# Four-layer convolution-style network: matmuls of different row or column tiles queued in groups, replicas in two-bank tiles, PSUM shared by both lanes

## The chip, the cores and the metric

The kernel runs on one core of a Trainium2 chip. The metric is the device time of one execution in microseconds; a kernel is run several times and the median counts. The engines are named as in the profile: PE (TensorE matmuls), PEld (TensorE weight loads), DVE (VectorE), ACT (ScalarE), POOL (GpSimd) and SP (the queue that issues DMA transfers). PSUM is the memory that PE writes; here it holds eight banks of 128 x 512 f32.

## What is computed

The input is 16 images of 56 x 56 positions and 128 channels in f32. Four layers follow one another, each of the form x = x + layer(group_norm(x)):

```
x = x + _L0_conv_ref(_gn(x), ...)   # shifted 7x7 window attention, 4 heads
x = x + _L1_conv_ref(_gn(x), ...)   # layer norm, gated products, l @ r over columns, layer norm
x = x + _L2_conv_ref(_gn(x), ...)   # Fourier layers: attention over heads, three spectral operators
x = x + _L3_conv_ref(_gn(x), ...)   # bilinear: depthwise convolutions and two contractions
```

The parts the change touches, cut to the core. Layer 3:

```
q = l2norm(xp[..., :NH*DK].reshape(b, t, h, NH, DK), -1).reshape(b*t*h, NH, DK)
K_H1 = conv2d(k, H1_w, groups=DK) ... + P1
kernel = jnp.einsum('xnk,xkd->xnd', q, K_H1)
V_G = conv2d(v, G_w) ... + I
feature = jnp.einsum('xvw,xvd->xwd', V_G, feature)
out = jnp.einsum('xnd,xvd->xvn', kernel, feature)
```

Layer 2, of which the change touches the scores over 32 heads, the product of the attention weights with values under a spectral filter, and the inverse transforms:

```
scores = jnp.einsum('bhtd,bhsd->bhts', qs, ks) / ...
out = jnp.einsum('bhts,bhsd->bhtd', softmax(scores), vs)
projd = _fno_layer(out, wP, wPs, bPs, (H, W))
```

Layer 1: two projections of the normed input, each gated by a sigmoid of a third and fourth.

## The kernel before

The image stays in SBUF as 128 channels by 3136 positions (`xt`) through all four layers; nothing but the table of layer 2, a padded copy of the keys and values of layer 3, input and output passes through HBM. The 16 images are written one after the other in the program text, the even ones on lane 0 and the odd ones on lane 1. A lane has its own work area (`arena`), small tiles and PSUM pools, so the framework's scheduler, which fixes the order of each engine's queue when the program is built, lets the two lanes run at the same time: it puts an instruction on its queue when its operands and its tile's buffer are ready by its own reckoning, the older image first. On the chip each queue then runs in that order, and an instruction that waits holds up what stands behind it on its engine.

PSUM before: each lane has two pools (`psp` and `prp`, lines 314 and 315) of two one-bank tiles. `psb` (line 333) takes from them alternately, or from the one that is asked for: in the bilinear stage the accumulators, convolutions and projections use pool 0 and the replicas pool 1.

Every f32 matmul stands in the profile as two LDWEIGHTS and two MATMUL records. A matmul whose operand has 32 rows uses a row tile of the array, and one whose output has 32 or 64 partitions a column tile.

The places that matter:

- `_bilinear`, stage 3, per image seven chunks of 448 positions. `contract` (line 1268 on) computes one of the einsums of layer 3 for a chunk; it is called three times a chunk, so 21 times an image. It runs in two halves `n`. In a half, four matmuls with 32-row operands (line 1277) spread rows of `y` over 128 partitions, the replicas; each replica is multiplied by `z` on DVE (line 1282), or, every third one, copied by ACT (line 1285) and multiplied on POOL (line 1286); then eight matmuls (line 1290), for `h` in two and `i` in four, add products `i` into the column tile 32 `i` of the accumulator. `conv` (line 1264) makes `z` by three matmuls per half of the outputs, and `project` the inputs of the chunk. The products have a ring of five buffers.
- `_fourier`, stage 2. In the loop of line 1086 on, for each of eight slices `q` of the spectrum, 16 pairs of heads are loaded from the table by two DMAs each on SP's queue into a ring of five buffers (line 1096), multiplied by the spectrum (line 1098; every third multiplication on POOL, the rest on DVE), and multiplied by the attention weights into two accumulators (line 1103), pairs with `half` 0 in the upper 64 partitions and `half` 1 in the lower. The accumulators stand from the first to the eighth step of a slice. In `attention` the scores are made by products (line 992, DVE or POOL) and matmuls (line 1001) in the same two halves. `inverse` (line 886) uses four column tiles.
- `_triangle`, stage 1: line 638 makes four columns of the gated projections in one bank, ACT takes the sigmoid (line 648), and DVE multiplies (lines 649 and 650).

Of the kernel before, what the change touches and what calls it, by code (L numbers as in the profile page):

```python
# [35 lines left out]
F32 = mybir.dt.float32  # L36
AF = mybir.ActivationFunctionType
ALU = mybir.AluOpType
# [258 lines left out]
def tile_blocks(ctx: ExitStack, tc: tile.TileContext, ins, out, at, stages=(0, 1, 2, 3)):  # L297
# [6 lines left out]
    def pool(name, bufs, **kw):  # L304
        return ctx.enter_context(tc.tile_pool(name=name, bufs=bufs, **kw))
# [7 lines left out]
    smp = [pool(f"small{k}", 8) for k in range(2)]  # L313
    psp = [pool(f"ps{k}", 2, space=PSUM) for k in range(2)]
    prp = [pool(f"pr{k}", 2, space=PSUM) for k in range(2)]

# [15 lines left out]

    def psb(which=None):

        count[0] += 1
        which = count[0] % 2 if which is None else which
        return (psp, prp)[which][lane[0]].tile([P, 512], F32, tag="ps", name=uid("psb"))

# [9 lines left out]
    ptt = nc.gpsimd.tensor_tensor  # L348
    act = nc.scalar.activation


# [234 lines left out]
def _triangle(env):  # L586
# [27 lines left out]
    def run(b, xt):  # L614
# [17 lines left out]
        for part in range(2):  # L632
            for g in range(T // 4):
                p = e.psb()
                for i in range(4):
                    c0 = (4 * g + i) * T
                    for half, w in ((0, "w1a"), (64, "w1b")):
                        mm(  # L638
                            p[half : half + 64, i * P : (i + 1) * P],
                            lhsT=xh[:, c0 : c0 + 64],  # L640
                            rhs=W(w).rearrange("p (k c) -> p k c", c=64)[:, :, HC * part : HC * part + HC],
                            start=True,
                            stop=True,
                        )
                pv = p.rearrange("p (i c) -> p i c", c=P)
                sg = e.w2()
                s3 = sg[:, :256].rearrange("p (i c) -> p i c", c=64)
                act(s3, pv[:, :, 64:128], AF.Sigmoid)
                tt(l3[:, 4 * g : 4 * g + 4, :], pv[:, :, 0:32], s3[:, :, 0:32], ALU.mult)
                nc.vector.scalar_tensor_tensor(  # L650
                    r3[:, 4 * g : 4 * g + 4, :], pv[:, :, 32:64], 1.0 / T, s3[:, :, 32:64], ALU.mult, ALU.mult
                )
            for g in range(4):
                for half in (0, 64):
                    p = e.psb()
                    s = slice(half, half + T)
                    for c in range(8):
                        mm(p[s, c * T : (c + 1) * T], lhsT=l3[s, :, 8 * g + c], rhs=r3[s, :, 8 * g + c], start=True, stop=True)
                    dst = ot[s, (4 * part + g) * CH : (4 * part + g + 1) * CH]
                    if half:  # L660
                        nc.scalar.copy(dst, p[s, :CH])  # L661
                    else:
                        nc.vector.tensor_copy(dst, p[s, :CH])
# [24 lines left out]
def _fourier(env):  # L688
# [183 lines left out]
    def inverse(parts, consume):  # L872
# [4 lines left out]
        for k in range(2):  # L877
            ng = 4 - k
            vs = []
            for u in range(2):  # L880
                p = e.psb()
                for i in range(4):
# [42 lines left out]
    def attention(uv, ar):  # L925
# [56 lines left out]
        for bank in range(2):  # L982
            sp = e.psb()
            for l0 in (0, 4):
                for c in range(2):
                    prods = []
                    for half in range(2):
# [10 lines left out]
                        prods.append(t4)  # L998
                    for l in range(4):
                        for half, t4 in enumerate(prods):  # L1000
                            mm(  # L1001
                                sp[64 * half : 64 * half + 64, :CH],
                                lhsT=xs[:, l0 + l, :],
                                rhs=t4[:, :, l, :],
                                start=l0 == 0 and c == 0 and l == 0,
                                stop=False,
                            )
            for half in range(2):
# [29 lines left out]
    def run(b, xt):  # L1038
# [47 lines left out]
        for q in range(8):  # L1086
            s = slice(q * STEP, (q + 1) * STEP)
            pa, pb = e.psb(), e.psb()
            acc = [pa[:, :STEP], pa[:, STEP : 2 * STEP], pb[:, :STEP]]
            for two in range(8):  # L1090
                prods = []
                for pair in (2 * two, 2 * two + 1):
# [5 lines left out]
                    engine().tensor_tensor(t3, x3[:, :, s], t3, ALU.mult)  # L1098
                    prods.append(t)
                for p, k, m in ((pa, 0, 2 * STEP), (pb, 2 * STEP, STEP)):  # L1100
                    for half, t in enumerate(prods):
                        pair = 2 * two + half
                        mm(  # L1103
                            p[64 * half : 64 * half + 64, :m],
                            lhsT=at[:, pair % 8, pair // 8, :],
                            rhs=t[:, k : k + m],
                            start=two == 0,
                            stop=two == 7,
                        )
            c0, o = e.w2(), e.w2()  # L1110
            nc.scalar.copy(c0[:, :STEP], acc[0])
# [58 lines left out]
def _bilinear(env):  # L1170
# [13 lines left out]
    def run(b, xt):  # L1184
# [12 lines left out]
        def project(q):  # L1197
# [4 lines left out]
            for t, o, m in ((ha, 0, 128), (hb, 128, 32)):  # L1202
                p = e.psb(0)
                mm(p[:m, :CH], lhsT=W("l3w1")[:, o : o + m], rhs=xg[:, :CH], start=True, stop=True)
                act(t[:m, :CH], p[:m, :CH], AF.Silu)
            p = e.psb(0)
            mm(p[:, :CH], lhsT=W("l3w2a")[:, :P], rhs=ha[:, :CH], start=True, stop=False)
# [4 lines left out]

            p = e.psb(0)
            for a in range(4):
# [19 lines left out]
            )  # L1234
            p = e.psb(0)
            for a in range(4):
# [19 lines left out]
        def conv(w, i, q):  # L1256
# [4 lines left out]
            for h in range(2):  # L1261
                p = e.psb(0)
                for dr in range(3):
# [4 lines left out]
        def contract(y, z, t):  # L1268

            acc = e.psb(0)  # L1270
            for n in range(2):
                done = []
                for two in range(2):
                    ps = [e.psb(1), e.psb(1)]
                    for i, p in enumerate(ps):
                        s = slice(64 * two + 32 * i, 64 * two + 32 * i + 32)
                        mm(p[:, :CH], lhsT=C("rep")[s, n * P : (n + 1) * P], rhs=y[s], start=True, stop=True)  # L1277
                    for p in ps:
                        d = prods[count[1] % 5].rearrange("p (h t) -> p h t", h=2)
# [7 lines left out]
                        done.append(d)  # L1287
                for h in range(2):
                    for i, d in enumerate(done):
                        mm(  # L1290
                            acc[32 * i : 32 * i + 32, :CH],
                            lhsT=C("red")[:, (2 * n + h) * 32 : (2 * n + h + 1) * 32],
                            rhs=d[:, h],
                            start=n == 0 and h == 0,
                            stop=n == 1 and h == 1,
                        )
            nc.scalar.copy(t, acc[:, :CH])
            return t

        def last(q, y):  # L1300
            y = contract(y, conv("l3wg", 1, q), e.w2()[:, :CH])
            p = e.psb(0)
            for a in range(4):
# [7 lines left out]
            )  # L1311
            p = e.psb(0)
            for a in range(4):
# [45 lines left out]
```

## Time and profile before

| what | value |
|---|---|
| runs, us | 20649.91, 20714.76, 20733.38 |
| median, us | 20714.76 |
| profiled execution, us | 20716.84 |
| its span, us | 20715.1 |
| mean granted TensorE clock | 0.807 |
| DVE products L1282 | x1792, 1913.2 us busy, 1089 ns each |
| POOL products L1286 | x896, 1887.4 us busy, 2106 ns each |
| ACT copies L1285 | x896, 476.0 us busy, 531 ns each |
| PE convolutions L1264 | 4032 records, 1877.7 us busy |
| POOL products L1098 | x688, 1167.8 us busy, 1699 ns each |
| DVE products L1098 | x1360, 1372.2 us busy, 1018 ns each |
| DMA arena<-table | x4096, 147.0 KB each |

A group of the profile is one line of the program on one engine: how many records, their busy time (the union of their intervals), the mean duration of one, and the idle time of the engine just before them with what ended most of it. Matmuls that run at the same time count once in the busy time, so busy time over count falls below the mean duration where they overlap. The granted clock is the share of TensorE's full clock that was allowed over a stretch.

After the first two images the program is periodic: two images, one of each lane, take some 2550 us. In the period from 10624 to 13174 us, lane 1 starts an image (window attention from 10624, triangle from 10921, attention of the Fourier layer from 11296, its products from 11420, the bilinear stage from 12406), and lane 0 is half an image ahead (Fourier products from 10647, the bilinear stage from 11402 to 12015, window attention of its next image from 12101, triangle from 12596, attention from 13059). These times are those of the lines 507, 638, 1001, 1103 and 1264 in the trace.

### The profile page before, as it was taken

The page shows a single profiled execution, that of the slowest core. Times are in us where ns is not written, and L with a number is a line of the kernel's source. Part 1 is how long each engine was busy: PE and PEld are TensorE (multiplying, and loading weights), DVE is VectorE, ACT ScalarE, POOL GpSimd, SP SyncE. Part 2 cuts the span into 40 slices and gives each one's busy share as a digit, 9 for nine tenths or more (in the row PEclk, how much of TensorE's full clock was granted, in tenths as well). Part 3 has the DMA queues.
Part 4 walks back from the last instruction along what each step waited for, and adds up shares of the span by engine and source line. Part 5 has one row for each costly group of instructions (what it writes and reads, how often), then busy time and mean ns, then how long its engine had stood idle before and what let it go on. Part 6 is the DMA issues. An engine that isn't in the chain of part 4 may idle for free. (4 is left out here: it accounts for less than half of the span.)

```text
span 20715.1 us, 240603 instructions
## 1 busy us (share of the span) xinstructions
PE 17351.0 (84%) x97248; PEld 8331.4 (40%) x97248; DVE 8795.3 (42%) x14107; ACT 4262.3 (21%) x7720; POOL 4451.6 (21%) x2924
## 2 busy tenths in 40 slices
PE   7888888888888798787987879878798787987968
PEld 4433345344353443534335343353433534334332
DVE  5543344443443434534354343543435434354332
ACT  2212222122121221212212122121221212212111
POOL 0232121221212212122121221212112121122211
PEclk7887888878878788787887878878788787887867
DMA  0220011110111101021010210202002010020100
GB/s 23 78 80 10 8 31 54 59 33 8 46 39 55 37 8 55 29 60 31 8 60 25 60 32 8 67 23 61 25 8 71 22 58 26 8 75 20 57 20 9
DMA packets 477330, 772.15 MB, mean 37 GB/s; under 512 B 118784, under 2 KB 220416, under 8 KB 475008
## 3 DMA queue, kind: packets, MB, share of 16 engines
q1 hardware_dynamic: 476080, 754.54, 12.1%
q8 instruction: 773, 12.66, 0.3%
q14 instruction: 333, 2.73, 0.0%
q10 hardware_dynamic: 144, 2.22, 0.0%
HBM read 709.84 MB, written 33.72 MB: 36 GB/s over the span
## 5 line engine op out<-in xcount | busy, mean ns | idle before, releaser
L1282 DVE TENSOR_TENSOR arena<-psb,arena 128x896 f32<-128x896 f32 x1792 | 1913.2, 1089 | 4070.5 <-PE psb L1277 2140.7
L1286 POOL TENSOR_TENSOR arena<-w,arena 128x896 f32<-128x896 f32 x896 | 1887.4, 2106 | 6633.9 <-ACT w L1285 3359.2
L1290 PE MATMUL psb<-arena,cst 128*32 128x448 f32 x10752 | 2954.4, 640 | 371.0 <-POOL arena L1286 351.7
L1103 PE MATMUL psb<-arena 112*64 112x448 f32 (+1 forms) x8192 | 2452.4, 521 | 379.0 <-DVE arena L1098 303.9
L1277 PE MATMUL psb<-arena,cst 32*128 32x448 f32 x5376 | 2490.3, 648 | 175.7 <-DVE arena L1282 100.2
L1264 PE MATMUL psb<-arena,wgt 113*128 113x448 f32 x4032 | 1877.7, 611 | 225.2 <-DMA arena<-table 149.0
L1098 POOL TENSOR_TENSOR arena<-arena 112x672 f32<-112x672 f32 x688 | 1167.8, 1699 | 3680.8 <-DMA arena<-table 3031.6
L1098 DVE TENSOR_TENSOR arena<-arena 112x672 f32<-112x672 f32 x1360 | 1372.2, 1018 | 1052.7 <-DMA arena<-table 990.9
L1103 PEld LDWEIGHTS psb<-arena 112*64 112x64 f32 x8192 | 887.2, 153 | 1745.2 <-issue 1011.0
L1277 PEld LDWEIGHTS psb<-arena,cst 32*128 32x128 f32 x5376 | 721.9, 202 | 1887.4 <-issue 1148.0
L1290 PEld LDWEIGHTS psb<-arena,cst 128*32 128x32 f32 x10752 | 508.7, 116 | 2401.4 <-issue 1421.6
L1264 PEld LDWEIGHTS psb<-arena,wgt 113*128 113x128 f32 x4032 | 813.5, 214 | 1225.5 <-issue 1097.4
L1285 ACT COPY w<-psb 128x448 f32<-128x448 f32 x896 | 476.0, 531 | 3226.9 <-PE psb L1277 3198.2
L821 POOL TENSOR_TENSOR arena<-arena,sm 128x448 f32<-128x448 f32 x560 | 609.6, 1123 | 1301.2 <-DVE sm L828 1126.4
L1001 PE MATMUL psb<-arena,standing 128*64 128x448 f32 x2048 | 573.7, 646 | 238.5 <-POOL arena L992 118.2
L857 PE MATMUL psb<-cst,arena 128*64 128x32 f32 (+1 forms) x10752 | 532.4, 274 | 237.5 <-DVE arena L865 65.6
L1265 ACT COPY arena<-psb 128x448 f32<-128x448 f32 x672 | 357.6, 532 | 1749.9 <-PE psb L1264 1749.9
L559 PE MATMUL psb<-cst,arena 128*49 128x128 f32 x2048 | 406.4, 356 | 290.6 <-DVE arena L554 207.2
L857 PEld LDWEIGHTS psb<-cst,arena 128*64 128x64 f32 x10752 | 515.7, 200 | 303.7 <-ACT arena L1155 70.6
L638 PE MATMUL psb<-wgt,arena 128*64 128x128 f32 x7168 | 615.2, 298 | 6.9 <-ACT arena L661 4.9
L505 POOL TENSOR_SCALAR arena<-xt,sm 128x21 f32<-128x21 f32 (+4 forms) x288 | 129.0, 460 | 2103.6 <-PE psb L524 1697.3
L992 DVE TENSOR_TENSOR arena<-w,coef 128x1792 f32<-128x1792 f32 x176 | 462.9, 2632 | 212.5 <-PE psb L1001 206.5
(265 smaller groups left out, 21242.9 us busy)
## 6 DMA issues: line engine op xcount, KB each, us to landing
arena<-table SPq DMA_DIRECT2D x4096, 147.0 KB
arena<-padded SPq DMA_DIRECT2D x1568, 38.4 KB
ld<-x SPq DMA_DIRECT2D x112, 224.0 KB
out<-w SPq DMA_DIRECT2D x112, 224.0 KB
arena<-arena SPq DMA_DIRECT2D x16, 784.0 KB
padded<-w SPq DMA_DIRECT2D x112, 56.0 KB
wgt<-wgt ACTq DMA_DIRECT2D x1, 2170.5 KB
cst<-cst SPq DMA_DIRECT2D x1, 2070.5 KB
```

Source lines behind the costliest of these rows:

```text
L638: mm(p[half : half + 64, i * P : (i + 1) * P], lhsT=xh[:, c0 : c0 + 64], rhs=W(w).rearrange("p (k c) -> p k c", c=64)[:, :, HC * part : HC ...
L821: ptt(d3[:, t, :], s3[:, t, :], bc(rs[:, t], 2, T), ALU.mult)
L857: mm(p[64 * c : 64 * c + 64, i * nl : (i + 1) * nl], lhsT=src[:, t * T : t * T + 64], rhs=fc[:, c], start=True, stop=True)
L1001: mm(sp[64 * half : 64 * half + 64, :CH], lhsT=xs[:, l0 + l, :], rhs=t4[:, :, l, :], start=l0 == 0 and c == 0 and l == 0, stop=False,)
L1098: engine().tensor_tensor(t3, x3[:, :, s], t3, ALU.mult)
L1103: mm(p[64 * half : 64 * half + 64, :m], lhsT=at[:, pair % 8, pair // 8, :], rhs=t[:, k : k + m], start=two == 0, stop=two == 7,)
L1264: mm(p[:, :CH], lhsT=W(w)[:, (2 * dr + h) * P : (2 * dr + h + 1) * P], rhs=rows[:, dr : dr + 8, :T], start=dr == 0, stop=dr == 2)
L1277: mm(p[:, :CH], lhsT=C("rep")[s, n * P : (n + 1) * P], rhs=y[s], start=True, stop=True)
L1282: tt(d, bc(p[:, :CH], 1, 2), z, ALU.mult)
L1285: nc.scalar.copy(r[:, :CH], p[:, :CH])
L1286: e.ptt(d, bc(r[:, :CH], 1, 2), z, ALU.mult)
L1290: mm(acc[32 * i : 32 * i + 32, :CH], lhsT=C("red")[:, (2 * n + h) * 32 : (2 * n + h + 1) * 32], rhs=d[:, h], start=n == 0 and h == 0, stop ...
```

## The change

PSUM is cut anew: one pool of four one-bank tiles and one of two two-bank tiles, for both lanes together.

```diff
-    psp = [pool(f"ps{k}", 2, space=PSUM) for k in range(2)]
-    prp = [pool(f"pr{k}", 2, space=PSUM) for k in range(2)]
+    ps1 = pool("ps1", 4, space=PSUM)
+    ps2 = pool("ps2", 2, space=PSUM)
...
-    def psb(which=None):
...
+    def psb():
+        return ps1.tile([P, 512], F32, tag="ps1", name=uid("psb"))
+
+    def psd():
+        return ps2.tile([P, 2, 512], F32, tag="ps2", name=uid("psd"))
```

A new function issues a group of matmuls: the first as it comes, the others with an ordering edge that keeps them behind the first on PE's queue. The edge is one of order alone; no one waits for the first to finish.

```diff
+    def together(group):
+
+        first, *rest = group
+        done = mm(**first)
+        with tc.issue_after(done.ins):
+            for kw in rest:
+                mm(**kw)
```

It is used in three places. In each the loop over tiles becomes the inner one and begins with the tile whose operand is made last in program order: `half` 1 before 0 in the scores and in the Fourier products, product 3 before 0, 1 and 2 in the contraction.

```diff
-                    for l in range(4):
-                        for half, t4 in enumerate(prods):
-                            mm(
+                    e.together(
+                        dict(
...
+                            rhs=prods[half][:, :, l, :],
...
+                        for l in range(4)
+                        for half in (1, 0)
+                    )
```

```diff
-            pa, pb = e.psb(), e.psb()
+            p2 = e.psd()
+            pa, pb = p2[:, 0, :], p2[:, 1, :]
...
+                group = []
                 for p, k, m in ((pa, 0, 2 * STEP), (pb, 2 * STEP, STEP)):
-                    for half, t in enumerate(prods):
+                    for half in (1, 0):
                         pair = 2 * two + half
-                        mm(
...
+                        group.append(
...
+                e.together(group)
```

```diff
-                    ps = [e.psb(1), e.psb(1)]
-                    for i, p in enumerate(ps):
+                    p2 = e.psd()
+                    for i in range(2):
                         s = slice(64 * two + 32 * i, 64 * two + 32 * i + 32)
-                        mm(p[:, :CH], lhsT=C("rep")[s, n * P : (n + 1) * P], rhs=y[s], start=True, stop=True)
-                    for p in ps:
+                        mm(p2[:, i, :CH], lhsT=C("rep")[s, n * P : (n + 1) * P], rhs=y[s], start=True, stop=True)
+                    for p in (p2[:, 0, :], p2[:, 1, :]):
...
-                for h in range(2):
-                    for i, d in enumerate(done):
-                        mm(
+                e.together(
+                    dict(
...
+                    for h in range(2)
+                    for i in (3, 0, 1, 2)
+                )
```

So the two replicas of a step of `two` lie in the two banks of one tile, and so do the two accumulators of a Fourier slice. Two more places use the two-bank tile: `inverse` puts the results of its two steps `u` in one, and the gated projections of the triangle go eight columns at a time instead of four, with one sigmoid and two multiplications of twice the length:

```diff
-            for g in range(T // 4):
-                p = e.psb()
-                for i in range(4):
-                    c0 = (4 * g + i) * T
+            for g in range(T // 8):
+                p = e.psd()
+                for i in range(8):
+                    c0 = (8 * g + i) * T
```

All other uses of `psb` take a tile of the common pool of four. The number and the shapes of the matmuls, the products and the DMAs stay as they are.

## The prediction

> **What bounds the kernel now.** I read the busy table first, then the stretches of one steady period, then the costliest groups, then the timeline. The profiled execution has a span of 20715.1 us and took 20716.84 us in all; the median of the runs shown is 20714.76, so a sum on this trace needs no correction. The chain of waits names less than a tenth of the span and decides nothing.
>
> ```profile
> PE 17351.0 (84%) x97248; PEld 8331.4 (40%) x97248; DVE 8795.3 (42%) x14107; ACT 4262.3 (21%) x7720; POOL 4451.6 (21%) x2924
> ```
>
> TensorE is twice as busy as any other engine. The busy time of two images (one of each lane), cut where a stage begins or ends, shows where that matters:
>
> ```profile
> 10624.00:11010.00 386.00, 330.29 (x2268) 183.03 (x2269) 201.91 (x342) 76.83 (x146) 88.10 (x66) 0.88 0.31 102
> 11010.00:11402.00 392.00, 290.47 (x2361) 191.76 (x2359) 199.45 (x318) 108.35 (x185) 73.38 (x57) 0.66 0.01 3
> 11402.00:12050.00 648.00, 582.13 (x1984) 200.05 (x1984) 224.73 (x295) 83.29 (x164) 184.26 (x99) 0.88 0.21 61
> 12050.00:12406.00 356.00, 257.70 (x2329) 177.79 (x2330) 180.94 (x340) 109.04 (x193) 65.18 (x70) 0.70 0.08 21
> 12406.00:13106.00 700.00, 644.30 (x3003) 261.61 (x3002) 243.51 (x418) 147.86 (x264) 123.70 (x63) 0.83 0.03 8
> 13106.00:13174.00 68.00, 49.78 (x214) 16.65 (x212) 41.22 (x47) 8.33 (x14) 22.10 (x11) 0.91 0.11 32
> ```
>
> Columns: stretch, its length, busy time of PE, PEld, DVE, ACT, POOL, granted clock, DMA share, GB/s. I call the rows A to F. In C (bilinear stage of lane 0 beside the Fourier products of lane 1) and E (bilinear of lane 1 beside triangle and attention of lane 0) PE is busy 90% and 92%, in A (Fourier products beside window attention) 86%: TensorE bounds these 1734 of 2550 us. In B and D it is busy 74% and 72% at a clock of 0.66 and 0.70: chains of short steps, no engine bound.
>
> ```profile
> L1290 PE MATMUL psb<-arena,cst 128*32 128x448 f32 x10752 | 2954.4, 640 | 371.0 <-POOL arena L1286 351.7
> L1103 PE MATMUL psb<-arena 112*64 112x448 f32 (+1 forms) x8192 | 2452.4, 521 | 379.0 <-DVE arena L1098 303.9
> L1277 PE MATMUL psb<-arena,cst 32*128 32x448 f32 x5376 | 2490.3, 648 | 175.7 <-DVE arena L1282 100.2
> ```
>
> These three lines hold 7897 of 17351 us, and none fills the array: 32 of 128 columns (L1290), 64 (L1103), 32 of 128 rows (L1277). Each f32 matmul stands as two records. The timeline shows what they cost alone and together:
>
> ```profile
> 10013.52 0.94 PE L1290 MATMUL psb<-arena,cst 128*32 128x448 f32 x2 [0.99 <-POOL arena L1286]
> ...
> 10014.39 1.01 PE L1277 MATMUL psb<-arena,cst 32*128 32x448 f32 x2
> ...
> 10016.21 1.02 PE L1277 MATMUL psb<-arena,cst 32*128 32x448 f32 x4
> ...
> 10018.24 1.69 PE L1290 MATMUL psb<-arena,cst 128*32 128x448 f32 x10 [1.00 <-POOL arena L1286]
> ```
>
> ```profile
> 10764.05 1.34 PE L1103 MATMUL psb<-arena 112*64 112x448 f32 x4 [0.93 <-DVE arena L1098]
> ...
> 10765.70 1.43 PE L1103 MATMUL psb<-arena 112*64 112x448 f32 x8 [0.31 <-DVE arena L1098]
> ```
>
> (start and length in us, engine, line, records, idle time before.) One L1290 matmul alone takes 0.94 us; five in a row (x10) take 1.69: four column tiles start within 20 ns and run together, and the fifth, on a tile already used, makes a second round. Two L1277 matmuls of different row tiles take 1.02 us against 1.01 for one, and both halves of an L1103 group 1.43 against 1.34 for one half. All at full clock. Concurrency is there whenever the matmuls stand next to each other; mostly they do not.
>
> **The change, part by part.** Per image a contraction runs 21 times in two halves, so 672 halves, 1344 replica pairs and 1024 Fourier groups in all.
>
> *Reduction, L1290.* Now 2954.4/672 = 4.40 us a half. Eight matmuls in a row on four column tiles are two rounds, what the x10 run took: 1.69 at full clock, 1.69/0.855 = 1.98 at the mean clock of C and E. Saves 2.42 x 672 = 1626 us. But the group is queued behind product 3, taken to be last, and every third product goes to POOL: over three halves the POOL products are number 2; 1; 0 and 3. In the first case number 2 needs a copy and POOL (531 + 2106 ns) against 1089 ns on DVE for number 3, so it is late by some 1.5 us and its two matmuls make two more rounds, or PE waits. 224 halves lose between 0 and 1.98 us; I take 1.98: 443 us. Net 1183, 74 per image.
>
> *Replicas, L1277.* Now 2490.3/1344 = 1.85 us a pair; in one two-bank tile both get their slot together: 1.02/0.855 = 1.19. Saves 0.66 x 1344 = 887, 55 per image.
>
> *Fourier products, L1103.* Now 2452.4/1024 = 2.39 a group; 1.43/0.88 = 1.63 at A's clock. Saves 0.77 x 1024 = 788, 49 per image: all in A for one lane, 42 in C and 7 in D for the other (436 and 76 of 512 records). What is late next is the slot: both buffers of a pair are freed at the group's end, and the sync queue's loads, which wait behind each other for free buffers, start then. A's DMA engines are used 31% of the time, so this costs latency in the ring of five buffers, which holds 2.5 groups; at A's 363 us for 64 groups a buffer has 14 us. No charge, bounded by A's whole gain.
>
> *Attention scores, L1001.* 573.7/128 = 4.48 us a group; four rounds are 1.69 + 2 x 0.75 = 3.19, /0.84 = 3.80. Saves 88 us, 5 per image.
>
> *Triangle gates and inverse transforms.* The same matmuls in larger tiles; the gates' ACT and DVE instructions are halved in number and doubled in length. Nothing: in E they lie beside PE's 92%; uncovered, the gates' 28 ACT instructions are 10.5 us an image.
>
> *The new wait.* Behind a group's first matmul stands everything queued on PE later, the other lane's matmuls too. Today's waits of PE on POOL at L1290 (351.7) and DVE at L1103 (303.9) bound it: 655 us if doubled, none if other work is ahead. *Shared PSUM.* Before, each lane had four banks of its own; now four single tiles and two pairs serve both. A Fourier accumulator keeps a pair for a whole step of 8 groups, 45 us in A, so in C replicas often have one pair left. No row shows this wait. From below: a gain, since conv and projection, which had two tiles together with the accumulator, may use four. From above: the last rival. I charge C for it in its busy share.
>
> **The sum, by stretch.** PE work after: A 330 - 49 = 281; C 582 - 74 - 55 - 42 = 411; E 644 - 129 x 640/672 - 5 = 516; D and B lose 7 and 5. At today's shares (86, 90, 92%) that is A 327, C 457, E 561, the far good end. Emptier PE also gets a lower clock: the rows have 0.88 at 90% busy, 0.70 at 72%. Between, I take 0.82 for C, 0.80 for E, 0.86 for A: 441, 535 and 288 us of work, and shares of 85, 90 and 85%: C 519, E 595, A 338. B, D and F are chains and stay 392, 356, 68. Sum 2268 of 2550 us, 0.889; times 20715 is **18,420 us**.
>
> The Trainium skill ("TensorE: Matmul & The Clock Gate", Part 1) speaks against this: half rate is the default, full rate is granted only after about 3.4 us of sustained activity and lost after an idle window. The trace agrees in kind: the grant falls with busy share, 0.88 to 0.66. By the rule taken strictly, groups with idle time between them would all run at half clock and the gain would be gone; by the rows it is a loss of 0.03 to 0.06 of clock.
>
> "TensorEngine Tiling (Array Packing)", PSUM Bottleneck, warns that packing speeds up the matmuls, not the evacuation behind them. The rows leave room: per half, DVE has 2.67 x 1.09 = 2.9 us of products and POOL 1.33 x 2.1 = 2.8, against 1.98 + 2 x 1.19 = 4.4 of PE.
>
> **Rivals.**
> 1. *The clock takes it back.* C, E and A fall to D's 0.70: work 411 x 0.88/0.70 = 517, 612, 353; over 85, 90, 86% it is 608, 680, 411. Sum 2515: **20,430 us**. For: B and D. Against: a slower PE is busier, and concurrent matmuls are denser activity; 0.66 comes in B, whose matmuls are short (L857, 280 ns).
> 2. *The chains bind.* E cannot end before lane 0's triangle and attention; C is held by one replica pair. If C and E keep half of my gain and A none: 584, 648, 386, sum 2434, **19,770 us**. For: DVE waits 2140.7 us for L1277, POOL 3359.2 for the copy behind it. Against: lane 1 did triangle and attention between 10844 and 11375, 531 us.
> 3. *Groups are torn.* The other lane's matmuls stand between, and runs stay as now: **20,700 us**, no change. Against: the members become ready together.
> 4. *Slower: one pair left in C.* Each of 84 replica pairs of an image waits for a reduction (1.69), a Fourier group (1.43), runs 1.02, then two products behind two of the other lane (2 x 1.09 + 2 x 1.02): 8.4 us, 702 for C; E, waiting for the triangle's pairs, gains nothing. 2550 + 54: **21,150 us**. It decides from 648/84 = 7.7 us a pair. For: a long-held pair. Against: one product in three leaves its bank after a 531 ns copy, and in E no accumulator holds a pair.
>
> **How the numbers follow.** Forecast 62% (17,300 to 19,100), rival 2 15%, rival 1 6%, rival 3 4%, rival 4 13%. Time 18,420. The low end is the far good end: 327 + 392 + 457 + 356 + 561 + 68 = 2161, 17,555, and 250 for freer PSUM in B and D. The high end takes in rival 2, 20,200; beyond it stay rivals 1, 3 and 4 and part of the low tail, some 2 in 10. About 0.5% is what a measurement tells from no change: faster 0.83, same 0.05, slower 0.12.
>
> **What would show it.** L1290 near 1330 to 1780 us busy, L1277 near 1600, L1103 near 1670, in runs of 16, 4 and 8 records; PE share below 84%; clock in the bilinear stretches 0.78 to 0.84. Wrong: runs of 2 as now (rival 3); the same work at a clock of 0.7 (rival 1); L1277 waiting for L1282 or L1285 through its tile, and a bilinear stretch beside the Fourier products of 650 us or more (rival 4).

## The result and the profile after

The changed kernel takes 24531.39 us (median of four runs, 24522.91 to 24558.7) against 20701.06 for the kernel before beside it: a ratio of 1.1855, interval 1.1828 to 1.1882. The forecast was 18420 us.

The busy table of the changed kernel, and the groups that answer to those shown of before. Lines have moved: the replicas are now L1293; every group's first matmul is recorded at L354 and the others at L357, told apart by shape (128*32 the reductions, 112*64 the Fourier products).

```profile
PE 16271.4 (66%) x97248; PEld 8569.4 (35%) x97248; DVE 8727.0 (36%) x13659; ACT 4155.1 (17%) x7424; POOL 4446.9 (18%) x2924
...
L354 PE MATMUL psd<-arena 112*64 112x448 f32 x2048 | 1657.0, 909 | 1262.3 <-POOL arena L1110 690.1
L357 PE MATMUL psd<-arena 112*64 112x224 f32 (+1 forms) x6144 | 2290.3, 657 | 0.0
...
L1293 PE MATMUL psd<-arena,cst 32*128 32x448 f32 x5376 | 1514.0, 697 | 875.4 <-DVE arena L1298 553.3
L357 PE MATMUL psb<-arena,cst 128*32 128x448 f32 x9408 | 1798.3, 777 | 0.0
...
L354 PE MATMUL psb<-arena,cst 128*32 128x448 f32 x1344 | 888.0, 754 | 476.7 <-DVE arena L1298 252.7
```

Most matmuls did what was forecast. Replicas fell from 2490.3 to 1514.0 us busy (forecast near 1600), and all 672 halves of the reductions stand as runs of 16 records; their two rows together cover 1803 us (forecast 1330 to 1780). The Fourier products did not: their two rows cover 2367 us against 2452.4 before, where 1670 was forecast. PE as a whole is 1080 us less busy, although the mean granted clock fell from 0.807 to 0.682 and a matmul takes longer on average (a record of the convolutions, which were not changed, 675 ns instead of 611). But PE is now idle a third of the time, and DVE, ACT and POOL are no busier than before: the time went into waiting. The idle time in front of the replicas rose from 175.7 to 875.4 us, that in front of the Fourier products from 379.0 to 1262.3.

Where the waiting comes from is seen as soon as one image is followed. These are the stretches of one image (length, busy time of PE, PEld, DVE, ACT, POOL, clock, DMA share, GB/s): load and window attention, triangle, triangle's end and Fourier attention, a gap, Fourier products, the rest of the Fourier layer, the bilinear stage, and the hand-over.

```profile
10761.00:10924.00 163.00, 102.08 (x890) 69.93 (x889) 72.00 (x133) 42.89 (x75) 6.78 (x20) 0.72 0.04 12
10924.00:11017.00 93.00, 73.30 (x725) 53.70 (x723) 40.67 (x92) 25.99 (x41) 0.11 (x1) 0.78 0.01 1
11017.00:11204.00 187.00, 125.27 (x846) 69.85 (x848) 73.56 (x104) 33.83 (x51) 32.06 (x13) 0.66 0.00 1
11204.00:11234.00 30.00, 15.41 (x96) 11.08 (x92) 8.55 (x10) 6.33 (x11) 1.05 (x1) 0.73 0.27 78
11234.00:11465.00 231.00, 152.28 (x560) 66.72 (x560) 90.92 (x105) 4.85 (x14) 74.12 (x48) 0.61 0.50 161
11465.00:11762.00 297.00, 160.92 (x1482) 120.00 (x1483) 111.90 (x208) 69.46 (x125) 47.26 (x45) 0.56 0.01 3
11762.00:12265.00 503.00, 370.34 (x1435) 137.21 (x1433) 138.43 (x194) 74.22 (x144) 109.99 (x53) 0.76 0.04 10
12265.00:12284.00 19.00, 12.08 (x55) 5.04 (x56) 6.99 (x7) 2.35 (x5) 6.35 (x5) 0.69 0.00 0
```

That is all the work there is in these 1523 us: one image, with PE busy 54% at a clock of 0.56 in the rest of the Fourier layer. Before, two images shared 2550 us. The timeline at the end of an image (start, length, engine, line) shows the next one waiting at the door:

```profile
12281.04 1.10 PE L1322 MATMUL psb<-cst,w 128*112 128x128 f32 x4 [0.71 <-ACT w L1315]
...
12281.93 1.06 PE L1333 MATMUL psb<-cst,xt 128*112 128x128 f32 x4
12282.18 1.09 DVE L1324 TENSOR_TENSOR w<-psb,arena 112x512 f32<-112x512 f32 x1 [7.83 <-PE psb L1322]
...
12282.78 1.70 PE L425 MATMUL psb<-cst,ld 112*128 112x112 f32 x8
```

L1333 is the last matmul of the older image, L425 the first of the next: its loading. So it goes at all fifteen borders: the first copy of an image's load stands at 1576, 3109, 4645, ..., the last convolution copy of the image before at 1557, 3090, 4626. On PE the two lanes do not overlap at all. In the kernel before, loading and window attention of an image ran while the image before was in its Fourier layer.

### The profile page after: what moved, and what is told of

The parts are those of the page before. It is cut to its first block, busy times and chain, and to the rows that moved or that the text cites. A ratio compares the mean times of both kernels' runs of the same rounds, so it can differ in the third digit from the quotient of the medians.

```text
span 24521.0 us, 241786 instructions
## 1 busy us (share of the span) xinstructions
PE 16271.4 (66%) x97248; PEld 8569.4 (35%) x97248; DVE 8727.0 (36%) x13659; ACT 4155.1 (17%) x7424; POOL 4446.9 (18%) x2924
## 5 line engine op out<-in xcount | busy, mean ns | idle before, releaser
L1298 DVE TENSOR_TENSOR arena<-psd,arena 128x896 f32<-128x896 f32 x1792 | 1881.6, 1086 | 4992.6 <-ACT arena L1281 2909.1
L1280 PE MATMUL psb<-arena,wgt 113*128 113x448 f32 x4032 | 2087.3, 675 | 801.7 <-DMA arena<-padded 801.7
L354 PE MATMUL psd<-arena 112*64 112x448 f32 x2048 | 1657.0, 909 | 1262.3 <-POOL arena L1110 690.1
L357 PE MATMUL psd<-arena 112*64 112x224 f32 (+1 forms) x6144 | 2290.3, 657 | 0.0
L1293 PE MATMUL psd<-arena,cst 32*128 32x448 f32 x5376 | 1514.0, 697 | 875.4 <-DVE arena L1298 553.3
L357 PE MATMUL psb<-arena,cst 128*32 128x448 f32 x9408 | 1798.3, 777 | 0.0
L354 PE MATMUL psb<-arena,cst 128*32 128x448 f32 x1344 | 888.0, 754 | 476.7 <-DVE arena L1298 252.7
L357 PEld LDWEIGHTS psd<-arena 112*64 112x64 f32 x6144 | 882.9, 208 | 827.9 <-issue 825.8
L1293 PEld LDWEIGHTS psd<-arena,cst 32*128 32x128 f32 x5376 | 439.4, 215 | 1953.5 <-issue 741.7
L354 PEld LDWEIGHTS psd<-arena 112*64 112x64 f32 x2048 | 303.4, 196 | 1773.9 <-POOL arena L1110 903.2
L1301 ACT COPY w<-psd 128x448 f32<-128x448 f32 x896 | 475.7, 531 | 1787.9 <-DVE arena L1298 1429.8
L567 PEld LDWEIGHTS psb<-cst,arena 128*49 128x49 f32 x2048 | 394.9, 200 | 843.1 <-issue 828.9
L357 PE MATMUL psb<-arena,standing 128*64 128x448 f32 x1792 | 681.7, 834 | 0.0
```

What stands on the lines that cost most here:

```text
L354: done = mm(**first)
L357: mm(**kw)
L567: nc.tensor.transpose(p[:WIN, i * P : (i + 1) * P], s3[:, 4 * g + i, :], C("ident"))
L1280: mm(p[:, :CH], lhsT=W(w)[:, (2 * dr + h) * P : (2 * dr + h + 1) * P], rhs=rows[:, dr : dr + 8, :T], start=dr == 0, stop=dr == 2)
L1293: mm(p2[:, i, :CH], lhsT=C("rep")[s, n * P : (n + 1) * P], rhs=y[s], start=True, stop=True)
L1298: tt(d, bc(p[:, :CH], 1, 2), z, ALU.mult)
```

## Experiments

*The theory.* The buffers of a pool are handed out in the order of the program text: a tile gets its buffer when the tile that had it one round earlier in the text is done. With one pool for both lanes, an image's first tile stands behind the last tile of the image before. *Rivals.* Too few banks, with long-held accumulators starving the other lane (the forecast's own slower case); or the groups themselves, whose first matmul holds up PE's queue. Every run was timed beside the kernel before; each ratio is to that, with its interval. That kernel took 20711, 20757 and 20716 us in the three rounds of runs, so a difference between kernels of different rounds is uncertain by some 50 us.

**PSUM split by lane again** (the changed kernel otherwise).

```diff
-    ps1 = pool("ps1", 4, space=PSUM)
-    ps2 = pool("ps2", 2, space=PSUM)
+    ps1 = [pool(f"ps1_{k}", 2, space=PSUM) for k in range(2)]
+    ps2 = [pool(f"ps2_{k}", 1, space=PSUM) for k in range(2)]
...
-        return ps1.tile([P, 512], F32, tag="ps1", name=uid("psb"))
+        return ps1[lane[0]].tile([P, 512], F32, tag="ps1", name=uid("psb"))
...
-        return ps2.tile([P, 2, 512], F32, tag="ps2", name=uid("psd"))
+        return ps2[lane[0]].tile([P, 2, 512], F32, tag="ps2", name=uid("psd"))
```

> The changed kernel with its PSUM split by lane again: two one-bank tiles and one pair for each lane, the same eight banks. Theory 1 (the tiles of a pool get their buffers in the order of the program text, so with one pool for both lanes an image's first tile stands behind the last tile of the image before it): the lanes overlap again, 16.5 to 18.9 ms, PE above 75% busy. Rival 2 (six tiles are too few for two lanes, a long-held accumulator starves the other lane): each lane now has fewer still, 21 to 25 ms. Rival 3 (PE waiting at a group's first matmul pushes the other lane out): stays near 24.5 ms.

20335.8 us, ratio 0.9825 (0.9791 to 0.986): 4196 us less than the changed kernel with the same eight banks, and fewer for each lane. PE is 77% busy and the images overlap again, as theory 1 says. The time misses theory 1's 16.5 to 18.9 ms by far, so a second loss is left.

**Sharing alone** (the kernel before with common pools, no groups and no pairs).

```diff
-    psp = [pool(f"ps{k}", 2, space=PSUM) for k in range(2)]
-    prp = [pool(f"pr{k}", 2, space=PSUM) for k in range(2)]
+    psp = pool("ps", 4, space=PSUM)
+    prp = pool("pr", 4, space=PSUM)
...
-        return (psp, prp)[which][lane[0]].tile([P, 512], F32, tag="ps", name=uid("psb"))
+        return (psp, prp)[which].tile([P, 512], F32, tag="ps", name=uid("psb"))
```

> The kernel before with nothing but its two pools made common to both lanes (4 and 4 one-bank tiles, no groups, no pairs). Theory 1: no overlap of images, slower than the changed kernel by what grouping saves on PE: about 26 to 28.5 ms. Rival 2: as many tiles as before and free for whoever needs one, 20 to 21.5 ms. Rival 3: no groups, so 20.7 ms.

23763.35 us, ratio 1.1481 (1.145 to 1.1513). No rival gives that: the banks are as many as before, there is no group, and the images stand one behind the other, some 1480 us each. The number was missed: I had taken the PE time that grouping saves to be lost here, but this kernel is 768 us faster than the changed one. With one lane at a time its Fourier products take 192 us an image from the first matmul to the last and the changed kernel's 231, the scores 52 against 68, the bilinear stage 534 against 502 between its first and last convolution copy. PE is idle 789.6 us in front of the Fourier products here and 1262.3 in the changed kernel. That a lane alone has nothing to put in front of a group's first matmul would explain this, but it is not shown: the two kernels also differ in how the banks are cut.

**Only the pairs shared** (the changed kernel with single tiles by lane).

```diff
-    ps1 = pool("ps1", 4, space=PSUM)
+    ps1 = [pool(f"ps1_{k}", 2, space=PSUM) for k in range(2)]
...
-        return ps1.tile([P, 512], F32, tag="ps1", name=uid("psb"))
+        return ps1[lane[0]].tile([P, 512], F32, tag="ps1", name=uid("psb"))
```

> The changed kernel with single tiles by lane (two each) and only the two pairs shared. Theory 1: an image goes ahead until its first pair, the triangle's gates, and stops there until the image before it has had its last pair, in the last contraction; what is hidden is loading, window attention and the first layer norm, some 260 of 1530 us an image: 19.5 to 21 ms, and no gate of an image before the last reduction pair of the image before. Rival 2: the lanes overlap, with long waits for pairs in the Fourier products; 17 to 19.5 ms with gates of one image in the middle of the other's bilinear stage. Rival 3: 24 ms.

22785.93 us, ratio 1.1008 (1.0978 to 1.1039). The time is above the 19.5 to 21 ms of theory 1: less is hidden than expected, 109 us an image and not 260. But the place is exact. The timeline of this kernel at the end of a bilinear stage:

```profile
12959.21 1.02 PE L1293 MATMUL psd<-arena,cst 32*128 32x448 f32 x4 [1.84 <-ACT w L1301]
...
12964.50 1.02 PE L1293 MATMUL psd<-arena,cst 32*128 32x448 f32 x4
12965.45 2.77 PE L646 MATMUL psd<-wgt,arena 128*64 128x128 f32 x42
...
12972.45 0.60 PE L1333 MATMUL psb<-cst,xt 128*112 128x128 f32 x4
```

The next image's first gate (L646, its first two-bank tile) starts 0.95 us after the last replica pair of the image before (L1293 at 12964.50), and before that image's last matmul (L1333), which uses a single tile. Everything of that image that comes before the gates had long been done: its window attention started at 11643, its layer norm ended at 11996. In the 969 us between lie the rest of the older image's Fourier layer and its bilinear stage. In one stretch of 70 us, from 12316 to 12386, the older image normalizes on DVE, ACT and POOL and no instruction touches a pair, and still no gate ran. Room is not what was missing, turn is. (Whether the framework's scheduler alone holds the turn, when it orders the queues, or the waits on the chip too, these runs do not tell apart.)

**The groups alone** (PSUM as before, replicas in single tiles as before).

> The kernel before with the three groups alone (scores, Fourier products, reductions), PSUM as before, replicas in single tiles. Theory 1: the part of the forecast that stands on grouping holds, 17.5 to 19.3 ms, with reductions in runs of 16 records. Rival 2: the same. Rival 3: slower than before, above 21 ms.

The edit is the function `together` and its three uses, as in the change. 19347.67 us, ratio 0.9347 (0.9322 to 0.9372). The groups are good. From the groups by line of this kernel:

```profile
L357 PE MATMUL psb<-arena,cst 128*32 128x448 f32 x9408 | 1569.1, 709 | 4.3 <-POOL arena L1300 4.3
L354 PE MATMUL psb<-arena,cst 128*32 128x448 f32 x1344 | 832.9, 710 | 358.7 <-POOL arena L1300 226.5 <-DVE arena L1296 129.4 <-DVE sm L391 1.9
```

First matmuls and followers run at the same time, so the rows may not be added; their union in the trace is 1574 us against 2954.4 before, inside the forecast's 1330 to 1780. Counted over the trace, 669 of the 672 halves stand as runs of 16 records, 2.34 us each on average (median 1.71, the forecast's two rounds at full clock). The Fourier groups are less whole: some 730 of the 1024 have all eight records together, and the others have matmuls of other groups between them.

**One group at a time.** First the groups without that of the Fourier products (its loop as in the kernel before), then that group alone.

> As the kernel with the three groups alone, but the Fourier products in their old order. Forecast's step (that group saves 49 us of PE an image and frees its buffers late at no cost): slower than 19348, at 19.7 to 20.2 ms. Rival (freeing two of five buffers together costs what the group saves): 19.2 to 19.5 ms.

> The kernel before with the group of the Fourier products alone. Forecast's step: 788 us of PE less, 20.0 to 20.4 ms. Rival (ring of five): 20.6 to 21.2 ms, with a Fourier stretch no shorter than before (363 us beside window attention, 660 beside the bilinear stage).

19573.27 us, ratio 0.9437 (0.9412 to 0.9463), and 20434.22, ratio 0.9848 (0.9825 to 0.9871). The first lies between its two expectations, the second 34 us above what the forecast's step gave. Reductions and scores bring 1184 us. The Fourier group brings 323 alone, and on top of the others 180 us when each kernel is set against the kernel before beside it (225 as the plain difference of medians). Alone it saves 584 us of PE, not 788. Its Fourier stretch takes some 327 us beside window attention and 666 beside the bilinear stage: the first is shorter than the 363 of before, the second no shorter than 660, as the rival had it. The scores save nothing on PE: 593.5 us in the first of the two kernels, 573.7 before.

**Eight buffers instead of five for the Fourier products**, once with the three groups and once without any.

```diff
-        slots = [ar[:TT, o : o + 3 * STEP] for o in (0, 672, 7224, 7896, 8568)]
+        slots = [ar[:TT, o : o + 3 * STEP] for o in (0, 672, 7224, 7896, 8568, 10312, 10984, 11656)]
...
-                    t = slots[n % 5]
+                    t = slots[n % 8]
```

> The three groups alone, with eight buffers instead of five for the Fourier products, in the lane's work area. Forecast's step (no charge for the ring): 19.2 to 19.5 ms, as with five. Rival (the ring of five binds): 18.5 to 19.1 ms and Fourier stretches shorter than 345 and 530 us.

> The kernel before with eight Fourier buffers instead of five, no groups. If it is the group (both buffers of a pair freed at its end) that made five too few: no gain, 20.6 to 20.8 ms. If five were too few anyway: 20.3 to 20.5 ms, the same 270 us as with groups.

With groups 19078.89 us, ratio 0.9193 (0.9172 to 0.9215); without 20474.36, ratio 0.9878 (0.9853 to 0.9903). The gain is 269 us with groups (315 against the kernel before beside each) and 241 without: five buffers were too few already, and whether grouping made it somewhat worse is within the noise. With groups the rival was right: its time came, and so did its Fourier stretches, some 338 and 435 us. The three groups with eight buffers are the fastest kernel of the study, faster than both the one before and the changed one.

**Replicas grouped in two single tiles.**

```diff
-                    for i, p in enumerate(ps):
-                        s = slice(64 * two + 32 * i, 64 * two + 32 * i + 32)
-                        mm(p[:, :CH], lhsT=C("rep")[s, n * P : (n + 1) * P], rhs=y[s], start=True, stop=True)
+                    rows = [slice(64 * two + 32 * i, 64 * two + 32 * i + 32) for i in range(2)]
+                    e.together(
+                        dict(out=ps[i][:, :CH], lhsT=C("rep")[rows[i], n * P : (n + 1) * P], rhs=y[rows[i]], start=True, stop=True)
+                        for i in (1, 0)
+                    )
```

> As the kernel with the three groups alone (19348 us), and the two replicas of a step grouped too, in two single tiles of the lane. Forecast's step (a pair costs 1.19 instead of 1.85 us and nothing else): L1291's place at 1500 to 1800 us busy instead of 2238, 18.6 to 19.1 ms. Rival (waiting for the second buffer of the pair costs as much): 19.2 to 19.8 ms.

20351.75 us, ratio 0.9804 (0.9782 to 0.9825): some 960 to 1000 us worse than the groups alone, beyond what even the rival gave. The replicas take 2602 us (the groups alone have 2363.6 there, not the 2238 of the expectation). It is no test of pairing, though: most replicas still stand alone in the trace (some 1400 runs of one matmul, and 457 of two against 489 in the groups alone), and only 263 halves of the reductions are whole, most others torn into runs of 6 and 10 records. Why the order came out so was not followed up.

**Pairing, step by step.** The groups alone with two single tiles a lane for everything but the replicas, and then the same with the replicas in one pair a lane.

```diff
-        which = count[0] % 2 if which is None else which
+        which = which or 0
```

```diff
-    prp = [pool(f"pr{k}", 2, space=PSUM) for k in range(2)]
+    ps2 = [pool(f"pr{k}", 1, space=PSUM) for k in range(2)]
...
-                    ps = [e.psb(1), e.psb(1)]
+                    p2 = e.psd()
+                    ps = [p2[:, 0, :], p2[:, 1, :]]
```

> The three groups alone, but everything outside the replicas takes its single tiles from one pool of two a lane, where the other stages had four (two pools in turn). If fewer tiles for the stages other than the bilinear one are what makes the lane-split change (20336 us) slower than the groups alone (19348 us): 19.9 to 20.4 ms. If not: 19.3 to 19.6 ms.

> As the kernel with two singles a lane, and the two replicas of a step in the two banks of one tile of the lane. Forecast's step (1.85 us a pair becomes 1.19, nothing else): 0.5 to 0.9 ms faster than the kernel with two singles. Rival (with one pair a lane no replica can be made until both products of the pair before have been read, so the DVE and PE turns no longer overlap): 0.2 to 1 ms slower than it.

19454.88 us, ratio 0.9394 (0.9366 to 0.9423), and 20119.71, ratio 0.971 (0.9677 to 0.9743). Fewer single tiles cost 107 us, so the second expectation holds. The pair costs 665, as its rival said, although it saves on PE most of what was forecast (575 of 887 us). The groups of the replicas, without and then with pairs:

```profile
L1291 PE MATMUL psb<-arena,cst 32*128 32x448 f32 x5376 | 2449.0, 663 | 251.8 <-DVE arena L1296 129.8 <-ACT w L1299 115.0
```

```profile
L1294 PE MATMUL psd<-arena,cst 32*128 32x448 f32 x5376 | 1874.0, 661 | 420.4 <-ACT w L1302 251.1 <-DVE arena L1299 163.4 <-DVE sm L406 4.0
```

And the longest waits in front of the products, in the same two kernels (who waited for whom, us in all, times, longest):

```profile
POOL arena L1300 <- ACT w L1299: 2931.0, 632, 65.0
...
ACT w L1299 <- PE psb L1291: 2685.0, 753, 10.5
```

```profile
POOL arena L1303 <- ACT w L1302: 5318.9, 717, 65.8
...
ACT w L1302 <- DVE arena L1299: 1194.4, 338, 14.4
```

PE saves 575 us on the replicas. But both banks of a pair are released by the later of two readers, so PE waits for readers longer (420 against 252 us), the copies now wait behind products, and POOL behind the copies. Most of PE's new idle time stands elsewhere, though: before the reductions (some 218 us more) and before the Fourier groups, again without and with pairs:

```profile
L354 PE MATMUL psb<-arena 112*64 112x448 f32 x2048 | 1225.0, 687 | 368.5 <-DVE arena L1108 158.3 <-POOL arena L1108 138.3 <-DMA arena<-table 57.6
```

```profile
L356 PE MATMUL psb<-arena 112*64 112x448 f32 x2048 | 1449.6, 802 | 782.3 <-POOL arena L1110 364.8 <-DVE arena L1110 311.8 <-DMA arena<-table 85.3
```

From the first to the last copy of the convolutions the bilinear stage takes some 706 us an image in both lanes, against 575 and 630 with single tiles, and the Fourier products some 304 us in both, against 340 and 535. So how the lanes lie beside each other changed too, and how much of the 665 us is the later reader and how much the new order of the queues is not shown; the replicas grouped in two single tiles, where only the order was changed, lost more than this.

**The late product first.** On the fastest kernel, the reduction begins with product 2 where that one goes to POOL.

```diff
+                late = 3
...
+                            late = 2 if len(done) == 2 else 3
...
-                    for i in (3, 0, 1, 2)
+                    for i in ((2, 0, 1, 3) if late == 2 else (3, 0, 1, 2))
```

> The three groups with eight Fourier buffers (19079 us), and a reduction's group begins with product 2 where that one goes to POOL (every third half), not with product 3. If PE stands in the middle of the group for the late product, as the forecast charged (up to 443 us in all): 18.7 to 18.95 ms. If the wait only moves to the group's first matmul: 19.0 to 19.2 ms.

19770.18 us, ratio 0.9532 (0.9505 to 0.9559): 691 us worse than the same kernel with product 3 first. Neither expectation had that. The first matmuls of the reductions, product 3 first and then product 2 first:

```profile
L354 PE MATMUL psb<-arena,cst 128*32 128x448 f32 x1344 | 871.4, 741 | 320.3 <-POOL arena L1300 239.1 <-DVE arena L1296 80.6
```

```profile
L354 PE MATMUL psb<-arena,cst 128*32 128x448 f32 x1344 | 963.7, 813 | 419.1 <-POOL arena L1301 401.5 <-DVE arena L1297 17.3
```

The wait in front of the group is 99 us longer in all and now mostly for POOL, and 547 halves instead of 669 stand as whole groups, so that the reductions cover 1999 us of PE in place of 1645. Why the groups were torn, and where the rest of the loss lies, is open.

## Why the prediction was wrong

The kernels lead from the one to the other in five steps, each a difference of measured medians, so that they add up by construction:

| step | us |
|---|---|
| kernel before | 20701 to 20757 |
| three groups | -1363 |
| single tiles of the other stages from one pool of two | +107 |
| replicas in one pair a lane | +665 |
| Fourier accumulators, inverse and gates in pairs too | +216 |
| pools common to both lanes | +4196 |
| changed kernel | 24531 |

A step's size depends on what stands before it: sharing costs 4196 us as the last step, and 3053 in the kernel before.

- **"Shared PSUM", bounded from below by a gain and from above by the last rival: this step failed.** I asked how many tiles there were and how long one is held, and took it that whoever is ready takes a free one. What decides is the order in which tiles get their buffers. With pools common to both lanes an image's first tile waits for the last tiles of the image before. I charged this nothing but a lower busy share of C; it cost 4196 us, 3053 without groups and pairs. The sign was in the program: each lane had its own pools. The price was not in the rows of before, where each lane stretches the other; the run with sharing alone gives it, some 1483 us an image one behind the other against 1275 with overlap. The last rival had the right side and the wrong mechanism, one pair left in one stretch, 21,150 us.
- **"Replicas, L1277", a saving of 887 us: right in kind on PE, wrong on the path.** PE's part was 575 us in the step where it was tried alone, and the time rose by 665. The step left out that two single tiles overlap the making of one replica with the reading of the other, and one pair does not; the waits agree with this, but a changed order of the queues is a rival that was not tested. The last rival's 8.4 us a pair is what the kernel with one pair a lane has, 706 us over 84 pairs. That is luck in part, since the rival's terms were for one pair left to both lanes.
- **"Reduction, L1290", net 1183 us, and "attention scores", 88:** 1271 forecast and 1184 measured for both. The mechanism is right for the reductions: the groups are whole, 2.34 us in place of 1.98, and their PE time fell by 1348 us, where 1626 was forecast before the charge for the late product. What that charge was really worth I cannot say: the run made to take it away lost 691 us. The scores' saving did not show on PE.
- **"Fourier products, L1103", 788 us:** mechanism right, size off. On PE the group saves 584 us alone, with some of the groups torn, and in time 323 alone and 180 to 225 on top. "No charge" for the ring is not contradicted (269 to 315 us gained by eight buffers with the group, 241 without), but the ring of five was too short with and without the group, which the sum did not see.
- **The clock.** The forecast lowered it by 0.02 to 0.06 in the bounded stretches; with the groups alone the mean is 0.769 and with eight buffers 0.778 against 0.807, about the loss assumed. The size came out better than its reason: "the grant falls with busy share" does not hold for all of the forecast's own rows (E 0.83 at 92%, F 0.91 at 73%). Nor did grouping bring PE to half clock, as the strict reading had it. In the changed kernel the clock cannot be the main cause: sharing alone, with a clock of 0.764, is slower than before by 15%, of which a clock lower by 0.807/0.764 would explain 5.6% at most (an estimate).
- **The wait at the group's head** was bounded by 655 us and charged nothing where other work is ahead. With two lanes the groups gain, with PE idle 352.4 us before the Fourier groups of the groups alone; with one lane at a time it is 1262.3 us in the changed kernel. That fits the condition "none if other work is ahead", since the change itself took that work away, but no run changes this condition alone.

By the Trainium skill ("TensorE: Matmul & The Clock Gate", Part 1) PE falls to half rate after an idle window. The changed kernel's stretch with PE at 54% ran at 0.56 of the clock, at half rate for 87% of it by the clock's records, which agrees; but the rule explains the rate of a matmul there, not why nothing else was running.

## What to carry to other kernels

Before pools of two independent streams are joined, ask in which order their buffers are handed out: if it is that of the program text, the streams run one after the other however many buffers are free. Queueing matmuls of different row or column tiles behind the last operand is worth 6.5% here by itself, with a second stream at hand to fill the wait. A tile of two banks frees both with the later reader, so two single buffers can be worth more than the concurrency that a pair buys on PE: here the pair saved 575 us of PE and the kernel lost 665. Small changes to the order of instructions moved this kernel by 700 to 1000 us, so a step is worth what its own run shows.

## What had not been expected of the hardware

The granted clock is lower where PE is idle more, but idle time alone does not give it. With the groups alone PE is busy 81% of the span in place of 84%, and the mean clock is 0.769 against 0.807; the changed kernel has 66% and 0.682. In its Fourier stretch, where the grouped matmuls of one image have nothing beside them, PE is busy 66% at 0.61 of the clock. But sharing alone, with no group, has 72% and 0.764, and the kernel with only the pairs shared, which has the groups and pairs, 71% and 0.708: about as much idle time, and a clock lower by 0.056. What else the clock answers to was not tested.
